# Five gathers in flight, another order of logits and weighting, and work passed from VectorE to ScalarE in a graph network on one core

## The chip, the cores and the metric

The kernel runs on one core of one Trainium2 chip. The metric is the device time of one execution in microseconds; lower is better. Engines are named as in the profile: PE is TensorE's matmul, PEld its weight load, DVE is VectorE, ACT is ScalarE, POOL is GpSimd and SP is SyncE, which here only issues transfers.

## The reference, cut to what matters

Four graph layers, each with a feed-forward layer behind it, on 3125 nodes with 256 features and 53125 edges sorted by destination. The first graph layer is an attention over edges and the second feed-forward layer is a choice of 2 of 8 experts; these two are concerned.

```python
# L0_gnn_ref: attention over edges, 8 heads of 32
q = (nfeat @ Wq.T).reshape(n, HEADS, HEAD_DIM) / SCALING
k = (nfeat @ Wk.T).reshape(n, HEADS, HEAD_DIM)
v = (nfeat @ Wv.T).reshape(n, HEADS, HEAD_DIM)
attn = jnp.einsum('ehd,ehd->eh', k[src], q[dst]) + attn_bias
m = jax.ops.segment_max(attn, dst, num_segments=n)
a = jnp.exp(attn - m[dst])
a = a / jax.ops.segment_sum(a, dst, num_segments=n)[dst]
out = jax.ops.segment_sum(v[src] * a[:, :, None], dst, num_segments=n)
x = x + out.reshape(n, FEAT) @ Wo.T
# L0_ffn_ref: a shared MLP and 4 small experts, all computed, 2 weighted in
h = relu(relu(x @ sW1 + sb1) @ sW2 + sb2) @ sW3 + sb3      # and the same form for each expert
# L1_ffn_ref: 8 experts, 2 for each row
h = gelu(jnp.einsum('end,edh->enh', layernorm(x) * ln_g + ln_b, W1) + b1)
y = jnp.einsum('enh,ehd->end', h, W2) + b2                  # two of the eight, weighted by softmax
```

## The kernel before

The nodes are 25 tiles of 125 (P and T). A program of one long stream is written in Python; a scheduling layer puts each engine's instructions into an order of its own, within the dependencies, so that the order on an engine is not that of the source. Every engine then works through its own order.

**The tile loop of the attention.** The edges of a destination tile lie in a window of 18 chunks of 128 edges (WC), handled as three parts of six (PC). For a part, `gathered` (L1648) fetches the k and v rows of the edges' sources from `kv_d` in DRAM into a buffer `kv`, by six indirect transfers of 128 rows of 2 KB, issued on POOL (L1653). Seven buffers rotate. A list `under_way` makes each gather wait until the one three before it has landed:

```python
if len(under_way) > 2:
    tc.add_manual_dep(got.ins, under_way[-3].ins.name, data_dep, reason="in turn")
```

For tile t the loop at L1908 runs the steps of two tiles side by side, `now` (t) and `before` (t−1), and prepares `after` (t+1). The steps:

- `one_hot` (L1790): DVE compares to give `oh`, edges by destinations (L282). `one_hot_turned`: PE turns it (L1819), ACT copies it out (`oht`, L1820).
- `queries` (L1802): PE makes the queries, ACT scales them into `q` (L1808), and DVE and ACT split them into three bf16 terms `q_t` (L1809 to L1812).
- `logits(s, p)` (L1824) for part p: PE spreads the queries over the edges, three bf16 matmuls a chunk, 18 a part (`qx`, L1833, two PSUM buffers); DVE multiplies them into the k half of `kv` two chunks at a time (L1836, three a part) and sums over the head (L1837).
- `sums_of` (L1841): DVE adds the edge bias (L1843), ACT takes an exp (L1846), PE sums over destinations (L1849), DVE copies the sums (L1851).
- `weights_of` (L1853): from those sums, DVE and PE make a shift for each edge (L1857, L1861, L1862, L1864), and ACT writes the weights into `kv` by an exp for each part (L1866).
- `weighted` (L1868): DVE multiplies v by the weights (L1871, three times), ACT turns `oh` into float32 (L1876, two buffers), PE adds up the destinations in `acc` (L1878, 18 matmuls a tile).
- `normed`, `normed_turned`, `projected` (L1882 to L1902): the count of edges goes to `deg` (L1883), the rest is divided, turned, multiplied by `wo` and added to `x`.

The source order in a turn of the loop is: logits of part 0 of `now`; weights and weighting of `before`; one-hot, norm and queries; logits of part 1; logits of part 2; projection; sums of `now`. Between them, calls of `beside()` put in steps of the first feed-forward layer (`experts0_by`, L814, two tiles a group, 13 groups), as far as tiles are done. Its ReLUs go through `relu_into` (L776), which takes DVE and ACT by turns, and its turned rows through `transposed` (L245), whose copies out of PSUM also take turns. From turn 5, each turn also advances `Windows`, which prepares count matrices for later layers with a few DVE and POOL instructions.

**The routed blocks.** `experts1` (L1092) runs 26 blocks of 256 rows (BLK). `run` (L1179) reads up to eight blocks' expert numbers into SP's registers and calls `block` (L1187) for each. A block loads its expert's weights on SP's queue into one of two slots `wslot`, gathers its rows `xs` on POOL (L1195), works out places and gates on DVE (L1200 to L1206), turns the rows (PE L1211, DVE L1213 to `xe`), multiplies them to `hid` (L266, ACT L1220) and by the second weights to `po` (L266), scales them (DVE L1225) and adds them to `x_d` in DRAM by an indirect transfer on POOL (L1226), which waits for the one before it.

Of the kernel before, what the change touches and what calls it, by code (L numbers as in the profile page):

```python
# [35 lines left out]
H, HD = 8, 32  # L36
# [34 lines left out]
def gnn_ffn_kernel(ctx: ExitStack, tc: tile.TileContext, a, out: bass.AP):  # L71
    nc = tc.nc
    data_dep = mybir.DependencyInfo(mybir.DependencyClass.Sync, mybir.DependencyReason.DATA)

    const = ctx.enter_context(tc.tile_pool(name="const", bufs=1, reuse_waits="tile"))
# [142 lines left out]
    turn = [0]  # L218
# [25 lines left out]

    def transposed(psum, dst, src, n, relu=False):  # L245

        for k in range(2):
            ps = psum.tile([128, 512], F32, name="tr")
            for i in range(n):
                nc.tensor.transpose(ps[:, i * P:(i + 1) * P], src[:, i, k * 128:(k + 1) * 128],  # L250
                                    ident[:P, :P])
            of = ps[:, :n * P].rearrange("f (i p) -> f i p", i=n)
            if not relu:
                evacuate(dst[:, k, :n, :], of)
            elif k:
                nc.scalar.activation(dst[:, k, :n, :], of, AF.Relu)
            else:
                nc.vector.tensor_scalar(dst[:, k, :n, :], of, 0.0, None, ALU.max)
# [516 lines left out]

    def relu_into(dst, ps, bias):  # L776
        turn[0] ^= 1
        if turn[0]:
            nc.vector.tensor_scalar(dst, ps, bias, 0.0, ALU.add, ALU.max)
        else:  # L780
            nc.scalar.activation(dst, ps, AF.Relu, bias=bias)
# [11 lines left out]
    class Experts0:  # L793


        def __init__(self, pools):
            pool = pools.enter_context(tc.tile_pool(name="ex0_b", bufs=1, side="right", reuse_waits="tile"))
            psum = pools.enter_context(tc.tile_pool(name="ps_ex0_b", bufs=1, space=PSUM, side="right",
                                                    reuse_waits="tile"))
            wpool = pools.enter_context(tc.tile_pool(name="w0", bufs=1, side="right", reuse_waits="tile"))  # L800
            with weights_of_pool(wpool, (SLOT0, D)):
                self.group = experts0_by(pool, psum, 2)
            self.now, self.left = iter(()), [(t0, min(2, T - t0)) for t0 in range(0, T, 2)]
# [9 lines left out]

    def experts0_by(pool, psum, most):  # L814

# [30 lines left out]
        def group(t0, n):  # L846
# [3 lines left out]
            lt = pool.tile([128, 2, most, P], F32, name="lt")  # L850
            transposed(psum, lt, ln, n)
            yield
# [3 lines left out]
            c = n * P  # L856

            def hidden(name, m, terms, bias):
                ps = tr()
                product(ps[:m, :c], terms)  # L860
                relu_into(name, ps[:m, :c], bias)

# [10 lines left out]
            for p in range(2):  # L873
                ps2 = psum.tile([128, 512], F32, name="pair", bufs=1)
                for j in range(2):
                    e = 2 * p + j
                    e1 = pool.tile([128, most * P], F32, name="e1")
                    hidden(e1[:, :c], 128, [(ew1[:, e, k, :], fan(lt[:, k, :n, :])) for k in range(2)],
                           cols[:, 3 + e:4 + e])
                    yield  # L880
                    product(ps2[j * 64:(j + 1) * 64, :c], [(ew2[:, e, :], e1[:, :c])])
                relu_into(e2[:, p, :c], ps2[:, :c], cols2[:, p:p + 1])
                ps = tr()
                product(ps[:, :c], [(pick[:, p, :], fan(gt[:, :n, :]))])
                nc.vector.tensor_mul(e2[:, p, :c], e2[:, p, :c], ps[:, :c])
                yield
# [205 lines left out]
    def experts1(route=None, ahead=lambda: None):  # L1092
# [5 lines left out]
        with ExitStack() as es:  # L1098
# [80 lines left out]
            def run(b0, n):  # L1179

                _, at = nc.values_load_multi_w_load_instructions(
                    block_e[0:1, b0:b0 + n], engines=[mybir.EngineType.SP], min_val=0, max_val=ne - 1,
                    skip_runtime_bounds_check_because="a count of 7 comparisons lies in 0..7")
                for b, e in enumerate(at):
                    block(b0 + b, e)

            def block(b, e):  # L1187
                wp = Packer()
# [19 lines left out]
                for k in range(2):  # L1208
                    ps = psum.tile([128, 512], F32, name="tr")
                    for r in range(R):  # L1210
                        nc.tensor.transpose(ps[:, r * 128:(r + 1) * 128],  # L1211
                                            xs[:, r, k * 128:(k + 1) * 128], ident)
                    nc.vector.tensor_scalar(xe[:, k, :], ps[:, :BLK], c[:, k:k + 1],  # L1213
                                            c[:, 2 + k:3 + k], ALU.mult, ALU.add)
                hid = pool.tile([128, 8, BLK], F32, name="hid")
                for m in range(8):
                    ps = psum.tile([128, 512], F32, name="hid_ps")
                    product(ps[:, :BLK], [(w1[:, k, m * 128:(m + 1) * 128], xe[:, k, :])
                                          for k in range(2)])
                    nc.scalar.activation(hid[:, m, :], ps[:, :BLK], AF.Gelu, bias=c[:, 4 + m:5 + m])  # L1220
                ys = pool.tile([128, R, D], F32, name="ys")
                for r in range(R):
# [4 lines left out]
                        out=x_d, in_=ys[:, r, :], in_offset=None, compute_op=ALU.add,  # L1227
                        out_offset=bass.IndirectOffsetOnAxis(ap=to[:, r:r + 1], axis=0))


# [389 lines left out]
    def attention(windows, experts):  # L1620
# [10 lines left out]
        with ExitStack() as es:  # L1631
# [16 lines left out]
            def gathered(at):  # L1648
# [3 lines left out]
                for c in range(PC):  # L1652
                    got = nc.gpsimd.indirect_dma_start(  # L1653
                        out=kv[:, c, KO:], out_offset=None, in_=kv_d,
                        in_offset=bass.IndirectOffsetOnAxis(ap=src_i[:, at + c:at + c + 1], axis=0))
                    if len(under_way) > 2:
                        tc.add_manual_dep(got.ins, under_way[-3].ins.name, data_dep, reason="in turn")
                    under_way.append(got)
# [143 lines left out]
            def queries(s):  # L1802
# [5 lines left out]
                nc.scalar.activation(q, ps, AF.Copy, scale=float(HD) ** 0.5)  # L1808
                nc.vector.tensor_copy(s.q[:, 0, :], q)  # L1809
                nc.vector.tensor_sub(q, q, s.q[:, 0, :])  # L1810
# [12 lines left out]

            def logits(s, p):  # L1824

# [3 lines left out]
                for c0 in range(0, PC, 2):  # L1829
# [5 lines left out]
                    k_ = kv[:, c0:c0 + 2, KO:VO]  # L1835
                    nc.vector.tensor_mul(k_, k_, ps)  # L1836
                nc.vector.tensor_reduce(  # L1837
# [30 lines left out]
            def weighted(s):  # L1868
                s.acc = psum.tile([P, 512], F32, name="acc", bufs=1)
                for p, kv in enumerate(s.kv):  # L1870
                    nc.vector.tensor_mul(  # L1871
                        kv[:, :, KO:VO].rearrange("p c (h d) -> p c h d", h=H),
# [9 lines left out]
            def normed(s):  # L1882
                nc.vector.tensor_copy(deg[:, s.t:s.t + 1], s.acc[:, H:H + 1])  # L1883
                inv = pool.tile([P, H], F32, name="inv")
# [23 lines left out]
            for t in range(T + 1):  # L1908
# [18 lines left out]
                if now:  # L1927
                    logits(now, 1)
                beside()
# [582 lines left out]
```

## Time and profile before

| | us |
|---|---|
| median of 3 runs (3419.65 to 3424.61) | 3423.1 |
| the profiled execution: its time, its span | 3426.26, 3424.4 |
| busy over the span: PE, DVE, ACT, POOL | 3136.0, 1740.3, 1031.9, 686.1 |
| first gather of the attention, last weighting matmul | 97.9, 923.4 |
| routed blocks: first and last `hid_ps` matmul | 1860.5, 2236.3 |

Times in the profile count from the span's start. A busy PE is a model for its ends, since matmuls are pipelined. A wait is idle time of an engine just before an instruction, put down to what released it last: `PE qx L1833 <- DVE kv L1836` reads as PE idle ahead of its matmuls of L1833 until DVE's L1836 was done. L266 is the line of the helper `product`, which records most matmuls, so its groups are told apart by the tile's name.

### The profile page before, as it was taken

To read this page: it belongs to the slowest core of one execution; us is meant where nothing else is said; L and a number is where in the kernel's file an instruction comes from. 1 tells how busy PE (TensorE), PEld (TensorE's weight loads), DVE (VectorE), ACT (ScalarE), POOL (GpSimd) and SP (SyncE) were. 2 spreads that over 40 slices of the span, in tenths; PEclk is the share of its full clock that TensorE was granted. 3 is DMA by queue.
4 is the path that set the end of the run, shared out by engine and by line. 5 is a ranking of instruction groups with operands and counts; after the bars stand their busy time and mean duration, and the time that the engine had idled before them with its cause. 6 is when DMAs were issued, how large, how long until landed. Compare 5 with 4: busy or idle time off the path is not lost. (4 is left out here: it accounts for less than half of the span.)

```text
span 3424.4 us, 45365 instructions
## 1 busy us (share of the span) xinstructions
PE 3136.0 (92%) x16587; PEld 2446.6 (71%) x16587; DVE 1740.3 (51%) x4905; ACT 1031.9 (30%) x1996; POOL 686.1 (20%) x639
## 2 busy tenths in 40 slices
PE   6688998998888899999996999979999999999898
PEld 2466776776677789898884888868755555578666
DVE  6477778787697534344674211145621111354672
ACT  1222222222255423232331222234422323332120
POOL 1575565565100000000133333200000000000000
PEclk9789999999989999999997999989999999999998
DMA  5766565555256734444344666654300000044101
GB/s 166 208 181 161 149 159 159 146 164 154 59 162 214 196 98 117 108 108 105 96 117 136 171 178 181 179 131 110 69 19 10 10 19 10 7 111 104 27 1 39
DMA packets 253209, 388.24 MB, mean 113 GB/s; under 512 B 41454, under 2 KB 201069, under 8 KB 252973
## 3 DMA queue, kind: packets, MB, share of 16 engines
q1 hardware_dynamic: 184090, 226.68, 23.9%
q0 software_dynamic: 54064, 141.25, 15.8%
q10 hardware_dynamic: 14819, 17.27, 1.9%
q8 instruction: 135, 2.21, 0.3%
q14 instruction: 101, 0.83, 0.1%
HBM read 314.47 MB, written 70.58 MB: 112 GB/s over the span
## 5 line engine op out<-in xcount | busy, mean ns | idle before, releaser
L2215 PE MATMUL agg<-cnt_f,hp 125*128 125x500 f32 (+1 forms) x3500 | 734.2, 369 | 23.1 <-ACT hp L2156 22.5
L2215 PEld LDWEIGHTS agg<-cnt_f,hp 125*128 125x128 f32 x3500 | 636.3, 189 | 104.5 <-ACT hp L2156 23.6
L1653 POOL DMA_INDIRECT kv<-kv_d,src_w x450 | 463.1, 1029 | 286.6 <-DMA kv<-kv_d,src_w 96.0
L2193 ACT CAST cnt_f<-blk 125x500 fp32r<-125x500 bf16 (+1 forms) x435 | 245.5, 565 | 520.0 <-PE agg L2215 495.5
L2193 DVE CAST cnt_f<-blk 125x500 fp32r<-125x500 bf16 (+1 forms) x440 | 185.3, 423 | 268.2 <-PE agg L2215 223.0
L1375 DVE SCALAR_TENSOR_TENSOR x<-po,gall,x 125x256 f32<-125x256 f32 x200 | 93.8, 484 | 417.4 <-PE po L266 416.9
L1369 ACT ACTIVATE h<-hid_ps,shift,scale 128x500 f32<-128x500 f32 (+1 forms) x224 | 161.7, 722 | 376.1 <-PE hid_ps L266 375.5
L1833 PE MATMUL qx<-q_t,oht 125*128 125x256 bf16 x1350 | 213.5, 294 | 57.2 <-DVE kv L1836 44.7
L1878 PE MATMUL acc<-kv,oh_f 128*125 128x265 f32 x900 | 229.2, 417 | 13.8 <-DVE kv L1871 13.8
L1878 PEld LDWEIGHTS acc<-kv,oh_f 128*125 128x125 f32 x900 | 181.3, 204 | 55.3 <-DVE kv L1871 18.3
L1833 PEld LDWEIGHTS <-oht 125*128 125x128 bf16 x1350 | 137.8, 105 | 103.0 <-issue 50.1
L266 PE MATMUL po<-wslot,h 128*125 128x256 f32 x800 | 203.0, 386 | 0.1
L266 PEld LDWEIGHTS po<-wslot,h 128*125 128x125 f32 x800 | 145.1, 187 | 75.2 <-ACT h L1369 27.0
L266 PE MATMUL hid_ps<-xe,wslot 128*128 128x256 f32 x832 | 194.0, 386 | 3.8 <-DVE xe L1213 3.5
L266 PE MATMUL hid_ps<-h,wslot 128*128 128x500 f32 (+1 forms) x448 | 193.4, 555 | 4.1 <-ACT h L1369 0.6
L1072 POOL DMA_INDIRECT xs_d<-r_l,pos x50 | 60.0, 1200 | 645.9 <-DVE r_l L1068 567.4
L266 PE MATMUL hid_ps<-v_rows,wslot 128*128 128x500 f32 (+1 forms) x448 | 186.8, 537 | 0.0
L1220 ACT ACTIVATE hid<-hid_ps,wslot 128x256 f32<-128x256 f32 x208 | 96.9, 474 | 295.8 <-PE hid_ps L266 295.8
L266 PE MATMUL po<-wslot,hid 128*128 128x256 f32 x832 | 184.4, 378 | 0.0
L266 PEld LDWEIGHTS hid_ps<-xe,wslot 128*128 128x128 f32 x832 | 149.0, 191 | 36.5 <-DVE xe L1213 6.1
L266 PEld LDWEIGHTS po<-wslot,hid 128*128 128x128 f32 x832 | 157.3, 189 | 22.9
L1836 DVE TENSOR_TENSOR kv<-kv,qx 128x512 f32<-128x512 f32 x225 | 150.8, 680 | 31.0 <-PE qx L1833 24.5
(512 smaller groups left out, 4611.3 us busy)
## 6 DMA issues: line engine op xcount, KB each, us to landing
wslot<-in_ex_W SPq DMA_DIRECT2D x52, 1024.0 KB
blk<-an_d SPq DMA_DIRECT2D x60, 546.9 KB
blk<-at_d SPq DMA_DIRECT2D x40, 546.9 KB
blk<-an_d SPq DMA_DIRECT2D x45, 410.2 KB
at_d<-ab SPq DMA_DIRECT2D x25, 683.6 KB
an_d<-an SPq DMA_DIRECT2D x25, 683.6 KB
blk<-at_d SPq DMA_DIRECT2D x30, 410.2 KB
kv<-kv_d,src_w POOLq DMA_INDIRECT x450, 3.7
```

The costliest lines, as they stand in the source:

```text
L266: nc.tensor.matmul(ps, l, r, start=(bias is None and i == 0), stop=(i == last))
L1072: st = nc.gpsimd.indirect_dma_start(out=xs_d, in_=l2[:, i, :].bitcast(I32), in_offset=None, out_offset=bass.IndirectOffsetOnAxis(ap=self.p ...
L1220: nc.scalar.activation(hid[:, m, :], ps[:, :BLK], AF.Gelu, bias=c[:, 4 + m:5 + m])
L1369: nc.scalar.activation(dst[:, m, :c], ps[:, :c], AF.Relu, bias=shift[:, l, col:col + 1], scale=scale[:, l, col:col + 1])
L1375: nc.vector.scalar_tensor_tensor(x[:, t0 + i, :], po, gating.all[:, t0 + i, e:e + 1], x[:, t0 + i, :], ALU.mult, ALU.add)
L1653: got = nc.gpsimd.indirect_dma_start(out=kv[:, c, KO:], out_offset=None, in_=kv_d, in_offset=bass.IndirectOffsetOnAxis(ap=src_i[:, at + c: ...
L1833: nc.tensor.matmul(ps[:, c, :], s.oht[:, p * PC + c0 + c, :], s.q[:, k, :], start=(k == 0), stop=(k == 2))
L1836: nc.vector.tensor_mul(k_, k_, ps)
L1878: nc.tensor.matmul(s.acc[:, :D + H + 1], of[:, c, :], kv[:, c, AO:VO], start=(p == 0 and c == 0), stop=(p == 2 and c == PC - 1))
L2193: to(f[:, :n, :], part[0][:, :n, m % MB, :])
L2215: nc.tensor.matmul(ps[f][:, :c], hp[:, m, k, f * 128:(f + 1) * 128], got[:, :c], start=(m == 0 and k == 0), stop=(m == T - 1 and k == 1))
```

## The change

There are four edits.

1. A gather waits for the one five before it to land.
2. In the loop, the multiplications of part 1's logits (L1836) are put behind the last L1871 of the preceding tile. This is a rule for the scheduling layer alone; it adds no wait on the chip, since both are DVE instructions.
3. In the steps inside the tile loop, all ReLUs of the feed-forward layer and the copies out of PSUM of its turned rows go to ACT, as do the first bf16 term of the queries and the copy of `deg`.
4. `block` is cut in two. `brought` loads, gathers and turns the rows of a block; `block` then does the products. Within a `run`, the block's second half calls `brought` for the next one between its `hid` and its `po` products. The first block of each `run` brings its own.

```diff
-    def transposed(psum, dst, src, n, relu=False):
+    def transposed(psum, dst, src, n, relu=False, to=None):
...
-                evacuate(dst[:, k, :n, :], of)
+                (to or evacuate)(dst[:, k, :n, :], of)
...
-    def relu_into(dst, ps, bias):
+    def relu_into(dst, ps, bias, on_act=False):
         turn[0] ^= 1
-        if turn[0]:
+        if turn[0] and not on_act:
...
-            transposed(psum, lt, ln, n)
+            transposed(psum, lt, ln, n, to=nc.scalar.copy if on_act else None)
...
+                last = None
                 for b, e in enumerate(at):
-                    block(b0 + b, e)
-
-            def block(b, e):
+                    last = block(last or brought(b0 + b, e), b0 + b + 1, at[b + 1] if b + 1 < n else None)
+
+            def brought(b, e):
...
+                return c, w1, w2, to, gate, xe
+
+            def block(got, b, e):
+                c, w1, w2, to, gate, xe = got
                 hid = pool.tile([128, 8, BLK], F32, name="hid")
...
                     nc.scalar.activation(hid[:, m, :], ps[:, :BLK], AF.Gelu, bias=c[:, 4 + m:5 + m])
+                following = None if e is None else brought(b, e)
                 ys = pool.tile([128, R, D], F32, name="ys")
...
+                return following
...
-                    if len(under_way) > 2:
-                        tc.add_manual_dep(got.ins, under_way[-3].ins.name, data_dep, reason="in turn")
+                    if len(under_way) > 4:
+                        tc.add_manual_dep(got.ins, under_way[-5].ins.name, data_dep, reason="in turn")
...
-                nc.vector.tensor_copy(s.q[:, 0, :], q)
+                nc.scalar.copy(s.q[:, 0, :], q)
...
-            def logits(s, p):
+            def logits(s, p, after=None):
...
-                    nc.vector.tensor_mul(k_, k_, ps)
+                    mul = nc.vector.tensor_mul(k_, k_, ps)
+                    if after is not None:
+                        tc.add_manual_dep(mul.ins, after.ins.name, in_order, reason="in turn")
...
-                    nc.vector.tensor_mul(
+                    s.last = nc.vector.tensor_mul(
...
-                nc.vector.tensor_copy(deg[:, s.t:s.t + 1], s.acc[:, H:H + 1])
+                nc.scalar.copy(deg[:, s.t:s.t + 1], s.acc[:, H:H + 1])
...
-                    logits(now, 1)
+                    logits(now, 1, before.last if before else None)
```

More of the change, by code (lines that the diff above doesn't have):

```diff
@@ L73, in gnn_ffn_kernel @@
     data_dep = mybir.DependencyInfo(mybir.DependencyClass.Sync, mybir.DependencyReason.DATA)
+    in_order = mybir.DependencyInfo(mybir.DependencyClass.NoSync, mybir.DependencyReason.SCHED_ONLY)
     const = ctx.enter_context(tc.tile_pool(name="const", bufs=1, reuse_waits="tile"))
@@ L801, in __init__ @@
             with weights_of_pool(wpool, (SLOT0, D)):
-                self.group = experts0_by(pool, psum, 2)
+                self.group = experts0_by(pool, psum, 2, True)
             self.now, self.left = iter(()), [(t0, min(2, T - t0)) for t0 in range(0, T, 2)]
@@ L812, in step, with experts0_by @@
             return False
-    def experts0_by(pool, psum, most):
+    def experts0_by(pool, psum, most, on_act=False):
         wp = Packer()
@@ L860, in hidden @@
                 product(ps[:m, :c], terms)
-                relu_into(name, ps[:m, :c], bias)
+                relu_into(name, ps[:m, :c], bias, on_act)
             s1 = pool.tile([128, 2, most * P], F32, name="s1")
@@ L881, in group @@
                     product(ps2[j * 64:(j + 1) * 64, :c], [(ew2[:, e, :], e1[:, :c])])
-                relu_into(e2[:, p, :c], ps2[:, :c], cols2[:, p:p + 1])
+                relu_into(e2[:, p, :c], ps2[:, :c], cols2[:, p:p + 1], on_act)
                 ps = tr()
```

## The prediction

> **What bounds the kernel now.** Lines are those of the kernel before. The diff touches two stretches, so I read them apart: the loop over 25 node tiles in `attention` (from 98 us, the first gather, to about 930) and the 26 routed blocks of `experts1` (1858 to 2240). First the busy time by stretch; columns: us, PE, PEld, DVE, ACT, POOL busy (instructions), granted clock, DMA share, GB/s.
>
> ```profile
> 160.00:925.00 765.00, 685.84 (x4462) 533.39 (x4462) 583.35 (x1282) 217.01 (x435) 437.38 (x422) 0.93 0.55 150
> 2000.00:2100.00 100.00, 98.58 (x463) 82.87 (x462) 19.75 (x64) 24.07 (x52) 34.18 (x27) 1.00 0.60 170
> 2100.00:2200.00 100.00, 98.82 (x462) 83.45 (x461) 17.96 (x58) 25.22 (x54) 34.03 (x27) 1.00 0.62 183
> ```
>
> The routed blocks keep PE busy for 98.7% of the time at full clock: nothing to win but 1.3%. The tile loop is different: 765 us for some 24 tiles, 31.9 us each; PE is busy 28.6 of them and DVE 24.3. PE idles 79 us and DVE 182. So I ask who waits for whom there (us in total, times, longest), first PE, then DVE, then POOL.
>
> ```profile
> PE qx L1833 <- DVE kv L1836: 30.2, 25, 1.8
> PE acc L1878 <- DVE kv L1871: 13.6, 21, 2.4
> PE tr L266 <- DVE lt L224: 6.4, 10, 0.8
> PE qx L1833 <- DVE q_t L1812: 5.7, 9, 0.7
> ```
> ```profile
> DVE q_t L1809 <- ACT q L1808: 27.6, 17, 2.4
> DVE kv L1836 <- PE qx L1833: 22.3, 32, 2.3
> DVE x L893 <- PE tr L266: 22.3, 13, 2.1
> DVE sums L1851 <- PE sm L1849: 18.3, 23, 1.9
> ```
> ```profile
> POOL kv L1653 <- DMA kv<-kv_d,src_w: 79.9, 134, 5.7
> POOL kv L1653 <- PE acc L1878: 67.4, 17, 11.6
> ```
>
> PE waits for DVE in all eight DVE rows of the full answer together 60 us, and for ACT 15. DVE never waits for a gather there: no such row. The gathers' 79.9 us of waiting in turn are on POOL alone. Only at the start (100 to 160 us) is DVE held by one:
>
> ```profile
> DVE kv L1836 <- DMA kv<-kv_d,src_w: 5.9, 3, 2.8
> ```
>
> Then the chain that the new order is about, in DVE's own sequence: the logits' sums (L1843, L1851), the weights (L1862, L1864), the weighting (L1871), with the next tile's logits (L1836, L1837) between them.
>
> ```profile
> 330.07 0.40 DVE L1843 SCALAR_TENSOR_TENSOR l<-l,eb_t 128x144 f32<-128x144 f32 x1
> ...
> 332.69 0.17 DVE L1851 COPY sums<-sm 125x8 f32<-125x8 f32 x1 [1.29 <-PE sm L1849]
> ...
> 335.40 0.30 DVE L1862 TENSOR_TENSOR l<-l,sm 128x144 f32<-128x144 f32 x1
> ...
> 342.00 5.08 DVE L1871 TENSOR_TENSOR kv<-kv 128x1536 f32<-128x1536 f32 x3
> ```
>
> From L1843 to L1871 it takes 11.9 us. ACT had ended the exps at 337.6: the rest of the wait is DVE finishing L1836, L242, L1837 and L224 in its queue. PE's 18 matmuls of L1878 come only behind the first L1871.
>
> **What the Trainium skill says.** "TensorE: Matmul & The Clock Gate", section "Architectural detail", calls the ACT and DVE queues strict FIFO. The trace agrees: DVE stood 2.35 us at L1809 (357.11), an L1836 behind it. The same page ("Part 1: The HAM clock gate") has PE's clock fall after idle stretches; here the loop is granted 0.93 and the gapless routed blocks 1.00. "DMA: Bandwidth & Descriptors", "Anatomy of one DMA — SWDGE (gpsimd) path", prices a POOL transfer at 2.0 us plus bytes/436e3: 2.6 us for 256 KB; the trace has 3.7 from issue to landing, which decides.
>
> **The change, part by part.**
>
> *Five gathers for three.* POOL issues one each 1.25 us (0.95 busy, 0.30 between). Three in 3.7 us is just that rate, so the wait binds only when landing is late. In the loop the gathers are ahead (no DVE row), so it is worth 0; POOL's next limit is a free `kv` buffer (67.4 us). At the start the 5.9 us go: −5. Bounds: −6, and +4 if five at once delay the weights that DVE awaits at 130 us (L834, 4.3 us seen).
>
> *Work from DVE to ACT.* Off DVE: 25 casts L1809 (0.29), 25 copies L1883 (0.15), 65 ReLUs of `relu_into` (0.47), 13 copies of `lt` (0.41): 7.3+3.8+30.6+5.3 = 47 us. On ACT: 25 casts (0.40, the row L1811), 25 copies (about 0.2), 65 ReLUs (0.47), 13 copies (0.36): 10+5+30.6+4.7 = 50 us. ACT goes from 28% to 35% of the loop; no function new to it, so no table load more. Queued behind ACT's new work are its casts `oh_f` (L1876) and `oht`; the former wait for PE anyway (209 us over the loop), which covers it. About 42 of the 47 us fall in the loop, 1.7 us a tile, and L1810 takes L1809's stall over, but now stands behind an L1836 and an L1837 (2.4 us), about what the stall was: its 27.6 us are largely filled. What of that reaches PE? At most the 60 us that PE waits for DVE. DVE idles 24% of the loop, so relief in front of such an idle is lost. I take half: −30. Bounds: 0 and −60, or −80 if PE's denser work lifts the clock as well.
>
> *Logits behind the weighting.* In the built order, PE has 32 and 36 of the 54 `qx` matmuls of a tile between the sums (L1849) and L1878 in the two tiles compared; afterwards 18 and 18. On DVE, part 1 (three L1836, one L1837: 3×0.68+1.75 = 3.8 us) moves behind L1871. The work is the same. The weighting starts up to 3.8 us sooner; behind it part 1 fills DVE's stalls on the queries and projections. During L1878 PE makes no `qx`, and two PSUM buffers allow DVE at most two L1836 there, so the L1837 that lay in that shadow in one of the two tiles is lost to it. Against it: PE's filler ahead of L1878 shrinks by 14 to 18 × 0.107 = 1.5 to 1.9 us. I take 0 for the order alone; bounds: +46 (24 × 1.9, all exposed) and −40 (DVE's stalls L893 and L1851 filled).
>
> *Routed rows a block ahead.* SP's order is untouched in this stage. On POOL the two gathers of `xs` stand as a pair ahead of a pair of scatters, not in between. On PE the four transposes move in front of `po`. What PE waits for in the whole stage:
>
> ```profile
> PE tr L1211 <- DMA xs<-xs_d,places: 21.9, 1, 21.9
> PE hid_ps L266 <- DVE xe L1213: 3.5, 6, 0.6
> PE tr L1211 <- DVE xe L1213: 0.5, 1, 0.5
> ```
>
> The first is the stage's start and stays. The others, 4.0 us, now have 7.1 us of `po` matmuls as cover: −3. DVE's L1213 now precedes L1225 and waits for `ec_d` (0.9 us a block, 21.4 in all); with the cover gone that would be +21. `tr` has two buffers and `xs` three, as before.
>
> Sum: −5−30+0−3 = −38. The profiled execution took 3426.3 us (span 3424.4), 3.2 above the median of the three runs shown; the profile's 3388 is 3385 against 3423.1.
>
> **The rivals.**
>
> *B, no limit moved.* Relief falls where DVE idles; the start and the routed blocks give −8 at most, or nothing: 3415 to 3423. For it: DVE idles 182 us already, and PE is 90% busy. Against: 60 us of named waits of PE for DVE.
>
> *C, the chain laid bare: slower.* Place: PE between L1849 and L1878. In a tile without expert products PE keeps there, after the change, 1.2 (L1849)+1.9 (18 `qx`)+0.6 (L1861)+1.6 (L250 and gates) = 5.3 us, while sums, two ACT steps, the weights and the first L1871 take, by their durations, some 8. If the missing 1.9 us show in all 24 tiles (+46) and half the relief (15) and the 8 are had: +23, 3446. It decides where the new wait ahead of L1878 passes 38/24 = 1.6 us a tile over today's 13.6/24 = 0.6. Against: today's 11.9 us are mostly queueing on DVE, and every other tile has expert products there.
>
> *D, more than the waits.* PE's waits for DVE nearly vanish (−60) and the clock goes from 0.93 to 0.95 (2% of 686, −14), start and routed −8: −82, 3341.
>
> *That the change does nothing* is excluded for the moves (the built program has them) but not for the gathers: in the loop the fourth and fifth may never be in flight.
>
> **How the numbers follow.** Forecast A 0.55 (3358 to 3408, its relief between a quarter and all), B 0.17, C 0.13, D 0.15. A difference of 0.2%, 6.8 us, is about what can be told here from no change. Faster by more: A, D and half of B, 0.78; same: 0.10; slower: most of C, 0.12. Range 3330 to 3422: 0.03 is left out below and about 0.14 above.
>
> **What would show it.** Right: L1833's wait for L1836 falls from 30.2 to about 15, DVE busy in the loop by about 42, the loop ends some 35 us earlier; the 5.9 us at the start are gone; `hid_ps` waits under 1 us for `xe`; POOL's 79.9 falls below 25 with no time of its own. Wrong: L1878's wait for L1871 grows from 13.6 past 50 (C), or DVE's idle grows by the 42 us while PE's stays at 79 (B). Gain from the blocks above 5 us would refute that part.

## The result and the profile after

The changed kernel took 3412.8 us (median of 9 runs, 3409.0 to 3417.9) against 3424.6 for the kernel before on the same chip (9 runs, 3419.4 to 3432.1): ratio 0.9969, 95% interval 0.9958 to 0.9979, some 11 us faster. 38 us had been forecast. The profiled execution took 3411.6 us (span 3409.8). Lines of the changed kernel are some ten higher: L1836 is now L1844 (the multiplication of the logits), L1878 is L1888 (`acc`), L1846 is L1856 (`el`), L1653 is L1661 (the gather).

The same stretches as before, first the tile loop, then two of the routed blocks (us, PE, PEld, DVE, ACT, POOL busy, clock, DMA share, GB/s):

```profile
160.00:925.00 765.00, 694.36 (x4509) 541.68 (x4507) 568.22 (x1186) 259.35 (x559) 415.53 (x414) 0.92 0.53 149
2000.00:2100.00 100.00, 99.41 (x473) 84.53 (x472) 20.09 (x63) 25.87 (x55) 36.14 (x28) 1.00 0.63 181
2100.00:2200.00 100.00, 99.41 (x473) 84.62 (x473) 19.87 (x62) 25.71 (x55) 32.06 (x24) 1.00 0.64 181
```

In the loop PE idles 70.6 us for 79.2 and does 1% more matmuls in the same time. (Not much should be made of that: the routed rows alone, below, leave the loop unedited, and PE idles 90.6 us there.) In the blocks it does 473 matmuls in 100 us for 463. Who waits for whom in the loop, PE first, then DVE, then POOL:

```profile
PE sm L1859 <- ACT el L1856: 17.3, 12, 3.2
PE tr L251 <- DVE ln L243: 16.1, 12, 2.2
PE pair L267 <- ACT e L782: 6.7, 14, 0.8
PE tr L251 <- ACT lt L255: 6.1, 12, 0.7
PE qx L1841 <- DVE kv L1844: 5.6, 4, 1.8
```
```profile
DVE kv L1844 <- PE qx L1841: 56.9, 61, 2.1
DVE oh L283 <- ACT oh_f L1886: 42.2, 18, 4.6
```
```profile
POOL kv L1661 <- PE acc L1888: 142.5, 22, 12.1
...
POOL kv L1661 <- DMA kv<-kv_d,src_w: 8.8, 29, 0.3
```

The wait that led PE's list, `qx` for DVE, went from 30.2 to 5.6 us. All rows of PE waiting for DVE together went from 60.4 to 29.6: the half that was forecast. But PE's waits for ACT rose from 14.6 to 36.3, above all for the exp `el`, which had no row of its weight before. DVE in turn waits more: 56.9 us for `qx` (22.3 before), and 13.1 us, in 15 pieces, for gathers, for which it had not waited in the loop before. POOL's wait in turn is nearly gone (8.8 us for 79.9) and has become a wait for a free buffer.

Where the 14.6 us of span came from, by milestones of the two traces: the first work after the loop and the feed-forward products left over from it (PE turning a weight slot) comes at 1127.4 for 1141.8 us, −14.4; the routed blocks take 368.9 us for 375.8, −6.9; the stretches between and behind them, which no edit touches, lost 6.7. The other traces, but for the last six runs, vary by about as much there: 717.6 to 723.0 us between, 1186.7 to 1192.2 behind. Up to the weight slot PE's busy time is 960.3 us for 962.1, so that the gain there is idle time, 167.1 us for 179.7.

### The profile page after: what moved, and what is told of

Read it like the earlier page. It is cut to its first block, busy times and chain, and to the rows that moved or that the text cites. A ratio compares the mean times of both kernels' runs of the same rounds, so it can differ in the third digit from the quotient of the medians.

```text
span 3409.8 us, 45330 instructions
## 1 busy us (share of the span) xinstructions
PE 3135.9 (92%) x16587; PEld 2449.4 (72%) x16587; DVE 1714.1 (50%) x4777; ACT 1075.6 (32%) x2124; POOL 672.7 (20%) x639
## 4 chain that ended last, share of the span: by engine, by line
PE 78%; DVE 7%; DMA 6%; issue 4%; ACT 3%; POOL 2%; SPq 0%; ACTq 0%; POOLq 0%; DVEq 0%
PE agg L2225 21%; PE po L267 19%; PE hid_ps L267 15%; PE acc L1888 6%; PE tr L267 4%; DMA kv<-kv_d,src_w 2%; PE qx L1841 2%; POOL kv L1661 2%; PE row L267 1%; PE tok L1537 1%; PE tr L251 1%; PE sm L267 1%; PE tr L2313 1%; PE pair L267 1%; PE p L267 1%
## 5 line engine op out<-in xcount | busy, mean ns | idle before, releaser
L1661 POOL DMA_INDIRECT kv<-kv_d,src_w x450 | 447.0, 993 | 277.4 <-PE acc L1888 142.8
L1888 PE MATMUL acc<-kv,oh_f 128*125 128x265 f32 x900 | 235.0, 426 | 5.9 <-DVE kv L1881 5.9
L1888 PEld LDWEIGHTS acc<-kv,oh_f 128*125 128x125 f32 x900 | 187.4, 210 | 46.8 <-DVE kv L1881 6.7
L1841 PE MATMUL qx<-q_t,oht 125*128 125x256 bf16 x1350 | 195.2, 282 | 17.7 <-DVE kv L1844 15.6
L1844 DVE TENSOR_TENSOR kv<-kv,qx 128x512 f32<-128x512 f32 x225 | 151.9, 682 | 72.1 <-PE qx L1841 59.0
```

Of the source, the lines that this page charges most:

```text
L1661: got = nc.gpsimd.indirect_dma_start(out=kv[:, c, KO:], out_offset=None, in_=kv_d, in_offset=bass.IndirectOffsetOnAxis(ap=src_i[:, at + c: ...
L1841: nc.tensor.matmul(ps[:, c, :], s.oht[:, p * PC + c0 + c, :], s.q[:, k, :], start=(k == 0), stop=(k == 2))
L1844: mul = nc.vector.tensor_mul(k_, k_, ps)
L1888: nc.tensor.matmul(s.acc[:, :D + H + 1], of[:, c, :], kv[:, c, AO:VO], start=(p == 0 and c == 0), stop=(p == 2 and c == PC - 1))
```

## The experiments

Theory after the result: the gathers and the routed rows made the gain, and the ACT edit and the order cancel. Rival: the ACT edit works as forecast, and the order takes it back. First, each edit alone on the kernel before, all four on one chip (before: 3429.4 us). Differences in us are the ratio's, times the time before.

**Five gathers.**

```diff
-                    if len(under_way) > 2:
-                        tc.add_manual_dep(got.ins, under_way[-3].ins.name, data_dep, reason="in turn")
+                    if len(under_way) > 4:
+                        tc.add_manual_dep(got.ins, under_way[-5].ins.name, data_dep, reason="in turn")
```

> The kernel before with the first edit alone: a gather waits for the one five before it. Theory 1 (relief in the tile loop was turned into new waits; the gathers help at the start only): 3 to 6 us less, the first one-hot after the start (the row at 159.3 us before) comes 4 us earlier as it did with all four edits (155.0), the loop's length otherwise unchanged; POOL's 79.9 us of waiting in turn go below 25 and turn into waiting for a free buffer. Rival (gathers in the loop are late and five of them are what made the whole gain): 10 to 12 us less.

Measured: 3416.5 us, 0.9963 (0.9948 to 0.9978), −12.7 us. At the start DVE's 5.9 us for a gather are gone, and the one-hot that DVE made at 159.3 us comes at 154.2. In the loop, POOL's waits with five gathers, then one of DVE's:

```profile
POOL kv L1653 <- PE acc L1878: 137.3, 22, 13.5
...
POOL kv L1653 <- DMA kv<-kv_d,src_w: 16.4, 31, 3.1
```
```profile
DVE win_f L2030 <- DMA win_src<-in_src,win_p: 0.8, 2, 0.4
```

Waits in turn fell from 79.9 to 16.4 us and buffer waits rose from 67.4 to 137.3, as forecast. Behind the last line may be something that the forecast missed: the transfers of `Windows` (`win_src`, `win_dst`, L2022) are issued by POOL too, among the attention's gathers. Before, DVE waited 7.8 us for them (5.6 for `win_src`, 2.2 for `win_dst`), now 3.5 (0.8 and 2.7). That this made the gain is not shown: the run with the routed rows alone, whose loop has three gathers as before, has 18.0 us of these waits and ends its loop no later.

**ACT alone.**

```diff
-                nc.vector.tensor_copy(s.q[:, 0, :], q)
+                nc.scalar.copy(s.q[:, 0, :], q)
...
-                nc.vector.tensor_copy(deg[:, s.t:s.t + 1], s.acc[:, H:H + 1])
+                nc.scalar.copy(deg[:, s.t:s.t + 1], s.acc[:, H:H + 1])
...
-        if turn[0]:
+        if turn[0] and not on_act:
...
+            transposed(psum, lt, ln, n, to=nc.scalar.copy if on_act else None)
```

> The kernel before with the third edit alone: ReLUs, turned rows, first query term and deg to ACT, the order and the gathers as before. Theory 1: DVE busy in the loop falls by 42 us, PE's waits for DVE fall from 60 to some 40, its waits for ACT rise from 15 to 25 or 30; 5 to 15 us less. Rival P (PE's own work is the limit and DVE's load does not count): within 4 us of before. Rival S (ACT's queue is what eats the gain): up to 10 us slower.

Measured: 3433.0 us, 1.0011 (1.0000 to 1.0022): nothing, or 4 us worse. DVE's and PE's waits in the loop:

```profile
DVE kv L1836 <- PE qx L1833: 54.9, 51, 3.0
DVE win_f L2030 <- DMA win_src<-in_src,win_p: 28.0, 4, 11.1
```
```profile
PE qx L1833 <- DVE kv L1836: 28.5, 26, 1.8
PE acc L1878 <- DVE kv L1871: 27.8, 9, 11.1
```

PE still waits 28.5 us for the multiplications (30.2 before). The relief went into DVE's own waiting. Four times DVE stood ahead of a window's rows, twice for some 11 us with a weighting (L1871) behind it in its queue: PE's 27.8 us for that weighting have the same longest wait. Such a stall need not come from the edit, since the unedited loop of the routed rows alone has one of 10.7 us.

**The order alone.**

```diff
-                    nc.vector.tensor_mul(k_, k_, ps)
+                    mul = nc.vector.tensor_mul(k_, k_, ps)
+                    if after is not None:
+                        tc.add_manual_dep(mul.ins, after.ins.name, in_order, reason="in turn")
...
```

> The kernel before with the second edit alone: part 1 of the logits behind the weighting. Theory 1: the chain from the sums to the weighting is laid bare, so PE's waits at L1849 for the exp of ACT (1.6 us before) and at L250 for the normalised rows (none for DVE before) rise to some 15 us each as with all four edits, while its waits for L1836 fall by 20 or more: 0 to 10 us slower, or even. Rival O (the order is what made the gain): 5 to 12 us less.

Measured: 3438.9 us, 1.0034 (1.0021 to 1.0047): 11.7 us slower by the ratio, 9.5 by the medians. In the 765 us of the loop PE does 4406 matmuls for 4462.

**Routed rows alone** (`block` cut in two, as in the change).

> The kernel before with the fourth edit alone: routed rows brought a block ahead. As predicted from the 4.0 us that PE waited for xe: 2 to 4 us less, the stretch from the first to the last hid_ps matmul (375.8 us before, 368.9 with all four edits) shorter by that. Rival: the 6.9 us by which that stretch shortened are all its own, 6 to 7 us less, the most part of the whole gain.

Measured: 3421.5 us, 0.9979 (0.9969 to 0.9988), −7.2 us. `hid_ps` runs from 1862.0 to 2231.4 us, 369.4 for 375.8. The waits for `xe` fell by 1.7 us only (to 1.8 and 0.5). The rest of the gain is in no row of waits, but in PE's busy time, which had hidden it: between the first and the last `hid_ps` the trace has 1728 matmuls in both kernels, and PE is busy with them for 367.6 us for 372.0.

This edit leaves the loop alone, and PE's order in it is that of the kernel before. Its line for the loop, beside the first line that the prediction shows, therefore tells how much two executions of one loop differ:

```profile
160.00:925.00 765.00, 674.40 (x4463) 525.68 (x4462) 584.52 (x1282) 217.19 (x435) 444.87 (x421) 0.95 0.55 149
```

PE did the same matmuls (4463 for 4462) in 674.4 us instead of 685.8, at a granted clock of 0.95 instead of 0.93, and idled 90.6 us instead of 79.2. Up to the weight slot it was busy 946.1 us for 962.1 and got there at 1141.0 us for 1141.8: 16 us of faster matmuls brought 0.8. In this pair of traces the speed of PE's matmuls did not set the loop, and a difference in PE's idle time of some 10 us is not yet an effect of an edit.

The four sum to −4.5 us where the whole change has some −11. The intervals of the four (3 to 5 us to either side each) are too wide to say from this that they do not add. The second set looks at sums of edits, and asks which engine's work sets the loop. On another chip (before: 3428.3 us):

**Everything but the order**, and **gathers and routed rows only.**

> The changed kernel without the new order: five gathers, ACT's ReLUs and copies, routed rows a block ahead. Before is about 3425 to 3429, the changed kernel stands at 0.9969 of before, the order alone cost +11.6. Theory A (the order takes back what the ACT edit brings): this kernel is 10 to 20 us faster than the changed one, near 3400, ratio 0.992; L1836's idle for PE on DVE stays near 57 us and PE's waits for DVE in the loop stay near 30 us. Theory B (relief of DVE reaches PE nowhere, with or without the order): it equals the kernel of gathers and routed rows alone within 4 us.

> The kernel before with five gathers and the routed rows a block ahead, and neither the ACT edit nor the order. The two parts touch different stretches, so their single gains should add: -12.7 and -7.2 give -20, ratio 0.9942, 8 to 10 us faster than the changed kernel. Theory A (the ACT edit with gathers in place brings about as much as the order costs): within 3 us of the changed kernel's time, because the gains alone share something. Theory B (ACT edit worth nothing, order costs 10): -20.

Measured: 3408.8 us, 0.9941 (0.9928 to 0.9954), and 3409.6 us, 0.9944 (0.9931 to 0.9957). Both beat the changed kernel (0.9969, 0.9958 to 0.9979): the intervals just part. The first was expected 10 to 20 us below it by theory A and is some 4 to 10; against the second it is equal: with gathers in place the ACT edit brings nothing. PE's waits in the loop of the first kernel; the one for the multiplications is still that of the kernel before, the one for the weighting is longer:

```profile
PE qx L1840 <- DVE kv L1843: 29.5, 25, 1.8
PE acc L1885 <- DVE kv L1878: 23.7, 12, 8.6
```

**Less work on DVE**, and **less work on PE**, each on gathers and routed rows. In the first the sum over a head takes 20 of its 32 products, in the second the third of the `qx` terms is left out.

```diff
-                    kv[:, :, KO:VO].rearrange("p c (h d) -> p c h d", h=H), AX.X, ALU.add)
+                    kv[:, :, KO:VO].rearrange("p c (h d) -> p c h d", h=H)[:, :, :, :20], AX.X, ALU.add)
```
```diff
-                        for k in range(3):
+                        for k in range(2):
...
-                                             start=(k == 0), stop=(k == 2))
+                                             start=(k == 0), stop=(k == 1))
```

> Gathers and routed rows as above, and the sum over a head's 32 products in the logits (the reduction after the qx products) takes only 20 of the 32: 75 reductions of 1.75 us become 1.1, so DVE has some 48 us less to do and no other engine has more. The output is not the reference's. If DVE's work reaches PE, as the forecast's half had it, it is 20 to 30 us faster than the kernel of gathers and routed rows. If DVE's work sets nothing in the loop: within 5 us of it, and DVE's idle grows by the 48.

> Gathers and routed rows as above, and the logits' qx products leave out the third of their three terms: 450 matmuls of 0.107 us, some 48 us less on PE and nothing less elsewhere; the output is slightly off the reference's. If PE's work sets the loop: 35 to 48 us faster than the kernel of gathers and routed rows. If DVE and PE take turns in setting it: 15 to 30, and as much for the run with less on DVE.

Measured: 3421.5 us (0.9976) and 3403.8 us (0.9922, 0.9909 to 0.9935). The first total misleads: with other values the router fills 28 blocks for 26. So I read where the blocks begin. The kernel of gathers and routed rows, then less DVE, then less PE:

```profile
L266 PE MATMUL hid_ps<-xe,wslot x832: 377/379/635, 1847.0 to 2216.3; 128*128 128x256 f32 x167
```
```profile
L266 PE MATMUL hid_ps<-xe,wslot x896: 377/379/635, 1813.5 to 2225.0; 128*128 128x256 f32 x180
```
```profile
L266 PE MATMUL hid_ps<-xe,wslot x832: 377/379/635, 1840.8 to 2209.7; 128*128 128x256 f32 x167
```

45 us less on DVE (75 reductions of 1.15 us for 1.75) bring the blocks 33.5 us earlier; 48 us less on PE bring 6.2. Read plainly, DVE's work in the logits' chain reaches PE, at 0.7 us for one, and PE's own hardly. But neither run changes the load alone. By the traces, 53% of DVE's instructions in the attention have another instruction just ahead of them than in the kernel of gathers and routed rows, where DVE has less to do, and 64% where PE has less. The clock that PE was granted in the loop moved as well, from 0.95 to 0.97 and to 0.89. Up to the weight slot PE is busy for 947.1 us in the kernel of gathers and routed rows, 928.4 with less DVE work, though its own work is the same, and 931.8 with less PE work. So the 0.7 is not shown to be the price of DVE's work by itself.

**The ACT edit's halves, its load by itself, and the order without it**, again with gathers and routed rows, on a third chip (before: 3427.4 us). The first two kernels move only the two copies of the attention, or only the ReLUs and `lt`. The third leaves every operation on DVE and also does it on ACT, into a tile `junk` that nothing reads:

```diff
+        if turn[0] and on_act:
+            nc.scalar.activation(junk[:ps.shape[0], :ps.shape[1]], ps, AF.Relu, bias=bias)
         if turn[0]:
             nc.vector.tensor_scalar(dst, ps, bias, 0.0, ALU.add, ALU.max)
...
                 nc.vector.tensor_copy(s.q[:, 0, :], q)
+                nc.scalar.copy(junk[:P, :D], ps)
```

> Gathers and routed rows, and of the ACT edit only the attention's own two copies (the cast of the queries, 25 x 0.29 us, and the degrees' copy, 25 x 0.15 us) on ACT: DVE 11 us less, ACT some 15 more. Taking 48 us off DVE's reductions alone brought the routed stage 33 us earlier, so 11 us less by itself would be worth 7. Theory A (the price of the ACT edit sits in ACT's queue, where the degrees' copy waits for the last weighted sum with the next tile's work behind it): this half of the edit is the bad one, 3 to 8 us slower than gathers and routed rows alone, ratio 0.995 to 0.997. Theory B (the price sits in the expert products, all of whose ReLUs now end on one engine): this half gains its 5 to 7 us, ratio 0.9925.

> Gathers and routed rows, and of the ACT edit only the expert products' ReLUs and the copies of lt on ACT: DVE about 31 us less in the loop, ACT about 31 more. Theory A: this half gains, 5 to 15 us faster than gathers and routed rows alone, ratio 0.990 to 0.993. Theory B: it loses what the other half gains, 3 to 6 us slower, ratio 0.995 to 0.996.

> Gathers and routed rows, with every operation of the ACT edit left on DVE and in addition done on ACT, into a tile that nothing reads (the same sources and sizes, the degrees' copy waiting for the weighted sum too): ACT's load of the edit without DVE's relief. DVE's relief and ACT's load then come apart: gathers and routed rows with the whole ACT edit took the same time as without it. If ACT's load is what cancels a relief of 15 to 25 us: 15 to 25 us slower than gathers and routed rows alone, ratio 1.000. If the relief is simply worth nothing in these operations: within 5 us, ratio 0.9945 to 0.996.

> The changed kernel without the ACT edit: gathers, the new order and the routed rows. The order alone cost 11.6 us on the kernel before; with the ACT edit and the gathers in place it cost 0.9969 less 0.9941, some 9.6. If its price doesn't depend on the others: 0.9944 + 0.003 = 0.9975, some 2 us slower than the changed kernel. If ACT's relief of DVE pays part of the order's bill (the rival that the two belong together): clearly slower than that, 0.999 or more.

Measured: 3408.3 us (0.9944, 0.9928 to 0.9960) and 3406.5 us (0.9940, 0.9925 to 0.9955): neither half does anything, so both theories on where the price sits fall. ACT's idle copies: 3369.8 us, 0.9835 (0.9818 to 0.9851). No theory had that: 128 useless operations on ACT (some 49 us of its time) make the kernel 37 us faster than without them, and it is the fastest kernel of this study. The change without the ACT edit: 3435.5 us, 1.0024 (1.0017 to 1.0032), clearly beyond the 0.9975 expected if the order's price were fixed. So the two edits do belong together. All four have gathers and routed rows, and each ratio is to the kernel before on the same chip:

| ratio to before | order as before | logits behind the weighting |
|---|---|---|
| work stays on DVE | 0.9944 | 1.0024 |
| work on ACT | 0.9941 | 0.9969 |

Under the new order the ACT edit is worth 0.0055, some 19 us; under the old one nothing. The order costs 27 us without it and some 10 with it. PE's waits without it, the first two rows:

```profile
PE qx L1841 <- DVE kv L1844: 38.9, 29, 1.8
PE tr L251 <- DVE ln L243: 19.3, 12, 2.9
```

What the kernel with idle copies has: the loop in three stretches, first gathers and routed rows, then with the copies (columns as above).

```profile
160.00:390.00 230.00, 201.14 (x1394) 157.03 (x1394) 182.39 (x383) 67.78 (x137) 144.23 (x143) 0.97 0.61 171
390.00:620.00 230.00, 208.52 (x1359) 162.42 (x1359) 178.27 (x388) 65.19 (x133) 132.59 (x129) 0.95 0.55 151
620.00:850.00 230.00, 208.73 (x1390) 162.83 (x1388) 181.03 (x407) 70.18 (x138) 136.24 (x137) 0.95 0.55 157
```
```profile
160.00:390.00 230.00, 208.02 (x1455) 163.32 (x1453) 191.19 (x400) 82.23 (x178) 152.44 (x147) 0.99 0.63 174
390.00:620.00 230.00, 215.57 (x1467) 167.99 (x1465) 188.42 (x416) 84.61 (x183) 147.10 (x143) 0.97 0.62 168
620.00:850.00 230.00, 214.88 (x1418) 167.68 (x1418) 188.48 (x418) 80.68 (x174) 126.44 (x123) 0.98 0.53 145
```

PE idles 51.5 us of the 690 for 71.6, at a clock some 2% higher, and PE's wait for the multiplications is 7.6 us for 30.9 with all of DVE's work in place. Its instructions also stand in another order: by the traces, 68% of DVE's instructions in the attention have another instruction just ahead of them than in the kernel without copies, and 12% of PE's matmuls. Nothing but the copies was edited, so it was they that made the scheduling layer choose another order. With the ACT edit the same count for DVE is 35%, with the order 59%; the gathers or the routed rows by themselves change some 1%, and nothing on PE. So in all kernels that move, add or leave out work in the loop, load and order had changed together. The last six runs were to part them: they hold each engine's instructions in a given order, whatever the load.

```diff
+    held = mybir.DependencyInfo(mybir.DependencyClass.NoSync, mybir.DependencyReason.SCHED_ONLY)
+    there = {i.name: i for i in tc.nc.cur_bb.bb.instructions}
...
+                    tc.add_manual_dep(now, before.name, held, reason="pinned")
```

> Gathers and routed rows, no ACT edit, no copies of it, but in the stretch up to the end of the loop every engine's instructions are held in the order that they have in the kernel with ACT's idle copies (0.9835). Theory O (the gain of that kernel is its order, that the scheduling layer chose because it reckoned with more work on ACT): 0.983, some 38 us faster than the same instructions in their own order (0.9944). Theory L (the extra work itself did it, by spacing what PE and DVE do): back at 0.994.

> The kernel with ACT's idle copies (0.9835), every other instruction held in the order of the kernel of gathers and routed rows (0.9944). Theory O: 0.994 to 0.997, the copies cost 0 to 10 us and the gain is gone. Theory L: still near 0.984.

> Gathers, routed rows and the whole ACT edit (0.9941 in the order that the scheduling layer gave it), with PE's, DVE's and the rest of ACT's instructions held in the order of gathers and routed rows alone (0.9944). This is the ACT edit as the forecast thought of it: 47 us off DVE, everything else where it was. If the forecast's step was right for a fixed order and the new order gave it back: 15 to 40 us faster, ratio 0.983 to 0.990. If relief of DVE in these operations is worth nothing: 0.994.

> Gathers, routed rows and the ACT edit, in the order of the kernel with ACT's idle copies, each moved operation standing on ACT where its copy stood. Theory O with a relief that is worth something: faster than that kernel (3370, 0.9835), by up to 30 us. Theory O with a relief worth nothing: 0.9835. Theory L: 0.994.

Measured: 3761.7, 3796.8, 3764.5 and 3765.0 us, ratios 1.0465, 1.0560, 1.0474 and 1.0476. But the kernel before took 3592.6 us beside them, 5% more than beside any of the runs above. Two were run again, on another chip:

> The bare kernel (gathers and routed rows) in the order of the kernel with ACT's idle copies, once more, since the kernel before itself took 3593 us beside it the first time, 5% above its usual time. Theory O (order): ratio 0.983, some 3370. Theory L (load): 0.994, some 3408.

> Gathers, routed rows and the ACT edit in that same order, once more. The difference from the bare kernel in that order is what the relief of DVE is worth when nothing else moves: the forecast's step would have it 15 to 40 us faster; a relief that the order had already made needless, within 5 us; a relief that lengthens the expert products' chain through ACT, slower.

Measured: 3763.6 and 3765.6 us, with the kernel before at 3596.2. In the trace of the bare kernel in the better order PE idles 237.1 of the loop's 765 us, 103.2 of them in one row of waits for nothing that the profile shows ("issue"), up to 11.1 us at a time. The routed blocks begin at 2204.8 us for 1847.0, and from there to the end it takes 1557.5 us, as it does without the hold (1559.2).

So what was lost there was lost in the stretch that was held. In all six the blocks begin at 2203 us or later, whichever order was held. It may be the hold itself that costs this; but the kernel before was slowed beside them too, and there is no trace of it to show where. I draw nothing on order or load from these six runs. They are inconclusive, and why they were slow was not found.

## Why the prediction was wrong

The direction was right and the time lies in the range, but 38 us were forecast and about 11 came. The two large terms, ACT's relief and the order, stood in the sum at −30 together; on top of gathers and routed rows they measured +9 (0.9944 to 0.9969). By the steps of the sum:

- **Five gathers, −5: measured −12.7** (−7.5 to −17.8). The 5.9 us at the start were right. POOL's 79.9 became 16.4 with this edit alone and 8.8 with all four, and with this edit alone the gathers in the loop were indeed ahead. The step "in the loop ... worth 0" failed: from the first weighting product to the weight slot the trace of this edit takes 983.5 us for 987.9. It asked only who waits for a gather; that POOL also issues the windows' transfers, for which DVE waited 7.8 us, it did not read. Whether those 4 us come from there stays open, for the reason given at the run. What is then left of the difference is inside the interval.
- **ACT relief, −30: measured +4 alone, 0 with gathers and routed rows, −19 with the order too.** The step that failed is "What of that reaches PE? ... I take half". It took PE's 60 us of waits as a stock from which any relief of DVE draws. Without the new order it drew nothing. From gathers and routed rows to the same with the ACT edit, PE's `qx` wait went from 30.9 to 29.5 us and DVE's wait for `qx` from 22.0 to 51.2. Up to the weight slot DVE's busy time fell by 35.2 us (845.6 to 810.4) and its idle time rose by 36.8 (281.6 to 318.4): what was freed became waiting. Why none of it reached PE is not shown, since the built order changed as well. The relief was also smaller than the 47 us of the prediction's sum. The rows that moved do have these durations (47 us on DVE, some 49 on ACT), but in the trace DVE's instructions overlap: the L1836 at 329.48 us takes 0.68, and the L1843 behind it starts at 330.07. A sum of mean durations counts such overlaps twice. The halving of PE's waits for DVE came true, but only under the new order, which cost as much as it brought, and 22 us of it came back as waits for ACT. The step had called ACT's queue covered by looking at `oh_f` alone, and the largest of these waits is for `el`.
- **Order, 0: measured +11.7 alone, +27 with gathers and routed rows, some +10 in the full change.** The step set the order to nought between bounds of +46 and −40; the runs give a cost in all three settings. Rival C, PE's shortened filler, explains a part of it. Between the sums and `acc`, PE has 28.0 `qx` matmuls a tile with gathers and routed rows, 11.7 with the order on top of these and 15.7 in the changed kernel (means of the first 24 tiles). PE's idle time in these gaps, over all tiles, is 41.9, 54.0 and 46.6 us: 12 of the 27 us. For the rest the runs name no single place; with the order and without the ACT edit, the rows of PE that grew most are the turned rows (none for DVE before, then 19.3) and the multiplications (30.9 to 38.9). The sign that the prediction named for C did not come: `acc` waited 13.6 us for the weighting before, 17.6 with the order alone and 3.1 in the changed kernel, where the lack showed at `sm` for `el` (17.3) and at the turned rows (16.1).
- **Routed rows, −3: measured −7.2.** The named waits fell from 4.0 to 2.3 us, where the forecast had 1. The prediction's own test was that a gain above 5 us would refute this part, and it does: the step "nothing to win but 1.3%" took PE's modelled busy time as work. The same 1728 matmuls were then busy for 4.4 us less.

So the two small terms, forecast at −8, came out at −20 by their single runs and −19 when measured together, and the two large ones together brought nothing. Of the rivals, B has its time nearly right (3415 to 3423) for a wrong reason, since PE's waits did move.

Three readings of the prediction were off without bearing on this. Forecast A, relief between a quarter and all, comes to 3355 to 3400 us from 3423.1, where it has 3358 to 3408. In C, 8 less 5.3 us is a lack of 2.7 us a tile and not of 1.9. And of the 4.4 us between ACT's exps and the weighting in the tile shown, DVE stood idle for 1.6 (0.74 for `qx`, 0.82 for turned rows), so that it was not all DVE's own queue.

Not settled: whether ACT's idle copies gain by the order that the scheduling layer chose or by the load itself. The change of order is shown, and that it is the cause is only argued. The same holds for the runs with less work on DVE and on PE.

## What to carry to other kernels

A wait of PE for DVE says that something in DVE's queue is late, not that any relief of DVE helps: ask whether the work to be taken away stands in the chain that PE waits for (45 us less of that went with 33.5, though order and clock moved too), or whether what is freed becomes idle time of DVE, as it did here. Where a scheduling layer sets the order, an edit of load is also an edit of order, and may be worth more by its order than by its load; compare the orders, and measure edits together as well as apart, since here ACT's relief paid only under an order that by itself was a loss. Before a difference in busy or idle time is put down to an edit, look at a kernel whose loop was not edited: here PE's idle time differed by 11 us between two such traces. Gathers and routed rows alone (0.9944) beat the full change (0.9969).

## What the runs showed that was not expected

- 128 operations added to ACT, some 49 us of work with no use, made the kernel 37 us faster than the same without them.
- 48 us less work for PE in the loop were worth 6 us. PE's clock in that stretch fell from 0.95 to 0.89, and up to the weight slot its busy time fell by some 15 us only (947.1 to 931.8), while its idle time rose from 180.1 to 189.8: most of what was saved went into slower matmuls. "TensorE: Matmul & The Clock Gate" of the Trainium skill ("Part 1: The HAM clock gate") has the clock fall after idle stretches. Beside gathers and routed rows (83.1 us of idle time in the 765 of the loop, clock 0.95), this kernel (97.1, 0.89) and the one with idle copies (65.6, 0.96) agree in direction. The kernel before and that with the routed rows alone do not: one loop, with 79.2 us of idle time at 0.93 and 90.6 at 0.95. So the amount of idle time alone does not tell the clock here.
- A PE that is busy by the profile for 98.7% of a stretch could still be made 1.8% faster there (368.9 us for 375.8): part of its busy time was not work. "Perfetto Trace Analysis" of the Trainium skill ("Tensor Engine Instruction (MATMUL, LD_WEIGHTS)") says that the end of such an instruction is estimated and not observed, so that its time in the profile is a model; the 1728 matmuls that took 372.0 us and then 367.6 agree with that.
